# Convolution weights of the second pass: widened on chip from their factors in place of a copy in DRAM

## The chip, the cores and the metric

The kernel runs on one core of a Trainium2 chip. The metric is the device time of one execution in microseconds, given as the median of several runs. The engines are called as in the profile: PE (TensorE matmul), PEld (TensorE weight load), DVE (VectorE), ACT (ScalarE), POOL (GpSimd) and SP (SyncE, which here issues every DMA, in order).

## The reference

Two layers run one after the other on an image `x` of shape (8, 256, 64, 64), all in float32: an attention over reduced keys and values, and a linear attention with a depthwise 5x5 convolution and a grouped 1x1 convolution in front of it. The second layer is what the change is about:

```python
def layer0(x):                       # heads 8, reduction 4
    xr = conv(x, w_sr, stride=4); xr = layernorm over channels
    q = w_q @ x;  k, v = split(w_kv @ xr)
    out = softmax(q k^T / sqrt(32)) v
    return x + gamma_s * (w_out @ out)

def layer1(x):
    qkv = w_qkv @ x                              # 768 channels
    dw  = depthwise 5x5 conv of qkv, padding 2   # w_dw
    agg = grouped 1x1 conv of dw                 # w_pw: 96 groups of 8 -> 8
    ms  = concat(qkv, agg).reshape(B, 64, 24, 4096)   # q, k, v of 8 channels a head
    q, k, v = relu(ms[:, :, :8]), relu(ms[:, :, 8:16]), ms[:, :, 16:]
    kv  = einsum(k, [v, 1]);  out = einsum(q, kv)
    out = out[:-1] / (out[-1:] + 1e-15)
    return x + batchnorm(w_proj @ out)           # 512 -> 256 channels
```

The depthwise and the grouped convolution together are one convolution within groups of 8 channels. Its weights are products: a depthwise tap times an entry of the small 8x8 matrix.

## The kernel before

A tile framework places tiles in pools, sets the semaphores and orders instructions of an engine by a plan of its own, except that those wrapped in `tc.keep_in_program_order` keep their written order. Every DMA goes through SP's queue, in order, with eight completion lanes: a transfer's issue waits for the one issued eight before it.

The kernel has three passes. `first_pass` (0 to about 1981 us) computes the first layer for eight images, 16 steps each, and the `qkv` of the second layer; its loop over `n` (L1056) interleaves by hand. It leaves in DRAM the `planes` (grids of 17x17 cells for the convolution), `kd` and `vd` (keys and values by token) and the image `x2d`. From step 17 on, each step also takes one step of the generator `conv_weights()` (L1112), which loads factors (`wd`, and `wsmall` once for all), forms sums of the four taps a cell (4 to 6 or to 9 variants, `n`), widens them by products on DVE (L698) and writes the wide weights `wt` to DRAM.

`second_pass` (to about 3015 us) runs over 64 units `u = (t, k, b)`: t in 2 halves, k in 4 parts, b in 8 images, with b innermost, so that eight units in a row (a group) share weights. For a unit it does, in the order of L1448 to L1512:

- loads: `load_tokens(u + 1)` (`kq`, 512 KB, and eight pieces of `vq`), in odd units `load_cells_q` (`d0`, two grids of 578 KB for a quad, that is a pair of units), later `load_cells(u + 2)` (`d1`, 578 KB).
- the convolution for keys, `convolve(u, i)` for i = 2, 0, 1: each eight matmuls (sixteen instructions) `cv<-w,c` at L1298 with the weights `w1` of 6 x 128 columns. i = 2 is copied by ACT (`both1`, L1307); for i = 0 and 1 DVE adds (`s`, L1314) and ACT applies the relu (`r`, L1315). Its inputs `c1` come from `paired(u + 1)` (two DVE subs and a copy on POOL), one unit ahead.
- the convolution for queries, `product(m, i, j)` for a quad of two units, nine products (`Q_ORDER`) over two units, two units later; inputs `across` (`c0`) and `down` (`y`), weights `w0` in two tiles: `w0_4` used in even units, `w0_5` in odd ones. The sums run on DVE, the relus on ACT.
- the sums for keys and values: `summed_raw`, `summed(u - 1)`, `ended_raw` and `ended`, with `reduced` (`red_raw`, `red_agg`, L1278 to L1280) on POOL ahead of the small matmuls L1408 and L1420.
- at the end `positive(u + 1)`: the relu of the next `kq` on ACT.

The weights `w1` of the next group come by four loads of 384 KB in its third to sixth unit (L1508); those of the queries by four and five loads of 256 KB at the end of the first two units of a group (L1511), after the old ones have been used. `third_pass` (to 3643 us) divides and projects; its first loads (`raw`) are issued in the last units.

Of the kernel before, what the change touches and what calls it, by code (L numbers as in the profile page):

```python
# [32 lines left out]
P = 128  # L33
# [533 lines left out]

def phase(dy, dx):

    return dy // 2 * 8 + dx // 2 * 4 + dy % 2 * 2 + dx % 2  # L570
# [4 lines left out]
def first_pass(ctx: ExitStack, tc: tile.TileContext, a, fine, planes, x2d, kd, vd, wtd):  # L575
# [7 lines left out]
    made = ctx.enter_context(tc.tile_pool(name="made", bufs=1))  # L583
# [19 lines left out]
    def load(src, name):  # L603
        consts[name] = (nilpool if name == "wsmall" else const).tile(list(src.shape), F32, tag=name, name=name)
        nc.sync.dma_start(consts[name], src)
# [24 lines left out]
    def load_consts():  # L630
        for n, src in (
            ("wq", a.w_q), ("wkv", a.w_kv), ("vec", a.vecs), ("gam", a.gamma_s), ("wout", a.w_out),
            ("wqkv", a.w_qkv), ("wsmall", a.w_small),
        ):
            load(src, n)
        combine_weights()
# [35 lines left out]


    def conv_weights():
        for j, half in ((j, half) for j in (2, 3, 0, 1) for half in range(2)):
            n = 6 if j > 1 else 9
            wd = made.tile([P, 8, n, 16], F32, tag="wd", name=f"wd_{j}_{half}", bufs=1)
            src = a.w_big[:, j, 8 * half : 8 * half + 8]
            nc.sync.dma_start(wd[:, :, :4], src.rearrange("p g (n f) -> p g n f", n=4))
            yield  # L680

            tc.keep_in_program_order(nc.vector.tensor_add(wd[:, :, 4:6], wd[:, :, 0:4:2], wd[:, :, 1:4:2]))
            if n == 9:
                tc.keep_in_program_order(nc.vector.tensor_add(wd[:, :, 6:8], wd[:, :, 0:2], wd[:, :, 2:4]))
                tc.keep_in_program_order(nc.vector.tensor_add(wd[:, :, 8], wd[:, :, 4], wd[:, :, 5]))
            for i in range(8):
                g = 8 * half + i
                w = made.tile([P, n, P], F32, tag="wb", name=f"wb_{j}_{g}", bufs=1)
                small_w = consts["wsmall"][:, j, g]
                if n == 6:  # L690
                    v = w.rearrange("p n (f o) -> p (n f) o", o=D1)
                    big = wd[:, i].rearrange("p n f -> p (n f)").unsqueeze(2).to_broadcast([P, n * 16, D1])
                    small_w = small_w.unsqueeze(1).to_broadcast([P, n * 16, D1])
                else:
                    v = w.rearrange("p n (o f) -> p n o f", o=D1)
                    big = wd[:, i].unsqueeze(2).to_broadcast([P, n, D1, 16])
                    small_w = small_w.unsqueeze(1).unsqueeze(3).to_broadcast([P, n, D1, 16])
                tc.keep_in_program_order(nc.vector.tensor_tensor(v, big, small_w, ALU.mult))  # L698
                if n == 6:
                    nc.sync.dma_start(wtd[j][:, g], w.rearrange("p n m -> p (n m)"))  # L700
                else:
                    nc.sync.dma_start(wtd[j][:, :, g].rearrange("n p m -> p n m"), w)
                yield
# [318 lines left out]
    weights = conv_weights()  # L1022
# [33 lines left out]
    for n in range(n_all + 6):  # L1056
        now, was = n < n_all, 0 <= n - 1 < n_all
        at = n % 16
        filled = now and n // 16 + 1 < B
        if filled and at == 5 and n > 16:  # L1060
            load_x(n // 16 + 1)
        if filled and at == 6:
            ahead = keys_values(n // 16 + 1)
        if now and at == (10 if n < 16 else 1):
            border(n // 16)

        if now:
            e0 = scores(*order[n], 0, q[n])
        catch_up()
        if was:  # L1070
            p = order[n - 1]
            for kc in range(2):
                valued(*p, kc, es[n - 1][kc])
            counted(*p, ej.pop(n - 1))
            es.pop(n - 1)
        if now:
            es[n] = e0, scores(*order[n], 1, q.pop(n))
            ej[n] = joined(*order[n], *es[n])
        if was:
            copied(*p)  # L1080
            normed(*p)

        products = todo.pop(n, [])
        taps = 2 if filled and 6 <= at < 10 else 0
        for f in products[:3]:
            f()
        if filled and at >= 10:
            next(ahead, None)
        for _ in range(taps):
            next(ahead)  # L1090
        if 0 < n + 1 < n_all:
            if n + 1 not in q:
                q[n + 1] = queries(*order[n + 1])
        for f in products[3:]:
            f()
        if was and p[2]:
            b, s = p[:2]
            pair = [att[b, s, 0], att[b, s, 1]]
            for oc in range(2):
                added(b, s, pair, oc)  # L1100
            if s % 2:
                differences(b, s // 2)
                rest_of = [f for pair in (1, 2, 0) for f in qkv_lazy(b, s // 2, pair)]
                for i, count in enumerate((7, 4, 7, 3)):
                    todo[n + 1 + i] = rest_of[:count]
                    rest_of = rest_of[count:]
        for _ in range(taps):
            next(ahead)
        if filled and at >= 10:
            next(ahead, None)  # L1110
        if n > 16:
            next(weights, None)  # L1112
    for _ in weights:
        pass
# [18 lines left out]
    (0, 0): 0, (0, 2): 1, (2, 0): 2, (2, 2): 3, (0, 1): 4, (2, 1): 5, (1, 0): 6, (1, 2): 7, (1, 1): 8,  # L1133
# [6 lines left out]
def second_pass(ctx: ExitStack, tc: tile.TileContext, a, planes, kd, vd, wtd, kvd, kvg, qd, ahead):  # L1140
    nc = tc.nc
    B = a.x.shape[0]
    def pool(name, bufs=1):
# [6 lines left out]
        pool("mid2"), pool("taps2"), pool("pairs2", 2), pool("sides2", 2), pool("between2", 2), pool("third2"),  # L1150
# [12 lines left out]
    wt, wq, grids, cells, kqs, vqs, quad = {}, {}, {}, {}, {}, {}, {}  # L1163


    def load_weights(u, g):
        t, k, b = units[u]
        if g == 0:
            home = second if k % 2 else first
            wt[t, k] = home.tile([P, 4, 6 * P], F32, tag=f"w1_{k % 2}", name=f"w1_{t}_{k}")  # L1170
        nc.sync.dma_start(wt[t, k][:, g], wtd[2 + t][:, 4 * k + g])

    def load_weights_q(u, which):
        t, k, b = units[u]
        home = w_q.tile([P, len(which), 4, P], F32, tag=f"w0_{len(which)}", name=f"w0_{t}_{k}_{len(which)}")
        for i, ij in enumerate(which):
            nc.sync.dma_start(home[:, i], wtd[t][Q_WEIGHTS[ij], :, 4 * k : 4 * k + 4])
            wq[t, k, ij] = home[:, i]
# [37 lines left out]
    def paired(u):  # L1216
        d = grids[u]
        c = pairs.tile([P, 3, 4, (NB + 1) * NB // 2], F32, tag="c1", name=f"c1_{u}")
        v = c.rearrange("p n g (y x) -> p n g y x", x=NB // 2)
        d0, d1, d2 = (d[:, :, :, i : i + NB - 1 : 2] for i in range(3))  # L1220
        nc.vector.tensor_sub(v[:, 0], d0, d1)
        nc.vector.tensor_sub(v[:, 1], d2, d1)

        nc.gpsimd.tensor_copy(v[:, 2], d1)
        cells[u] = c
# [25 lines left out]
    for g in range(4):  # L1251
        load_weights(0, g)
# [37 lines left out]
    def convolve(u, i):  # L1290
        t, k, b = units[u]
        c, w = cells[u], wt[t, k]
        ps = bank("cv", f"cv1_{u}_{i}", 5)
        for g in range(4):
            for da in range(2):
# [4 lines left out]
                    c[:, i, g, cols],  # L1300
# [144 lines left out]

    positive(0)
    paired(0)
    for u in range(n_all + 3):  # L1448
# [16 lines left out]
        if conv and u % 2 == 0:  # L1465
            across(q // 2, 0)
            down(q // 2, 1)
        if now:
            convolve(u, 2)
        if u + 1 < n_all:  # L1470
            paired(u + 1)
# [8 lines left out]
        products(u, 0)  # L1480
        if now:
            convolve(u, 0)
        if conv and u % 2 == 0:
            down(q // 2, 0)
            across(q // 2, 2)
        products(u, 1)
        if now:
# [3 lines left out]
        if now:  # L1491
            ended_raw(u)
            convolve(u, 1)
        if u + 2 < n_all:
            load_cells(u + 2)
        if u == 0:
            load_tokens(2)
            load_weights_q(0, Q_ORDER[:4])
            load_weights_q(0, Q_ORDER[4:])
# [320 lines left out]
def kernel_body(ctx: ExitStack, tc: tile.TileContext, a, out):  # L1820
# [21 lines left out]
    wtd = [scratch(f"wt_{j}", [P, 16, 6 * P] if j > 1 else [9, P, 16, P]) for j in range(4)]  # L1842

    first_pass(tc, a, fine, planes, x2d, kd, vd, wtd)
    with ExitStack() as held:
        top = held.enter_context(tc.tile_pool(name="top3", bufs=1, side="right"))
        ahead = third_pass(held, tc, a, planes, x2d, kvd, kvg, qd, out, top)
        second_pass(tc, a, planes, kd, vd, wtd, kvd, kvg, qd, ahead)
# [125 lines left out]
```

## Time and profile before

| what | value |
|---|---|
| median of 3 runs | 3652.02 us (3647.74 to 3656.05) |
| the profiled execution, its own time | 3644.77 us |
| its span in the profile | 3642.9 us |
| mean granted TensorE clock | 0.986 |
| DMA over the span | 706.47 MB, mean 194 GB/s |
| second pass, copies `both1` of units 0 to 3 | 1985.4, 1993.1, 2011.5, 2030.6 us |
| the same, units 11, 12 | 2150.4, 2175.9 us |
| the same, units 19, 20 | 2278.1, 2301.1 us |
| the same, units 27, 28 | 2401.9, 2425.2 us |
| the same, units 59, 60, 61, 62, 63 | 2902.5, 2915.3, 2937.6, 2953.3, 2968.3 us |
| clock records at 0.5 within the second pass, from | 1976.8, 2004.1, 2021.2, 2171.3, 2297.6, 2543.4, 2792.6, 2918.9, 3000.8 us |

The starts of L1307 are the clock of the second pass: one a unit, in order, so that the distance of two is the time of a unit. Busy shares over the whole span mix three passes with different limits; only windows within a pass tell what limits it. A DMA share near 1 means that all 16 DMA engines have a packet under way.

### The profile page before, as it was taken

The numbers are of one execution on the slowest core, as the hardware profiler recorded it, in microseconds if no ns is written. First come the engines' busy times: TensorE is split into PE (matmuls) and PEld (weight loads), VectorE is DVE, ScalarE is ACT, GpSimd is POOL, SyncE is SP. The second block draws the span as 40 slices with busy tenths as digits, with TensorE's granted clock in tenths as the row PEclk, the third lists the DMA queues.
The fourth block names the chain that finished last, engine by engine and source line by source line (L and its number), as shares of the span: only waits on it lengthen the run. The fifth ranks groups of instructions, "written<-read, shape, count | busy, mean of one in ns | idle before, by whom it ended". The sixth has DMA issues, their size and how long they took to land.

```text
span 3642.9 us, 64216 instructions
## 1 busy us (share of the span) xinstructions
PE 3544.9 (97%) x24738; PEld 1944.9 (53%) x24738; DVE 2270.6 (62%) x3395; ACT 1319.4 (36%) x2729; POOL 1544.4 (42%) x1490
## 2 busy tenths in 40 slices
PE   8999999999999999999998999999999999999998
PEld 4443534434435344344334888888888873333333
DVE  1567576576685766655766767676776684454442
ACT  2445344453453443544443222222322323333322
POOL 2434343344342433433443656565665541222222
PEclk9999999999999999999999999999999998999999
DMA  5346546555575564443465999999999988787773
GB/s 181 101 109 170 149 123 180 145 164 161 141 197 152 136 197 134 134 132 100 124 172 144 292 276 272 286 288 276 279 288 284 273 243 238 217 238 229 219 216 98
DMA packets 629449, 706.47 MB, mean 194 GB/s; under 512 B 81680, under 2 KB 487696, under 8 KB 629136
## 3 DMA queue, kind: packets, MB, share of 16 engines
q1 hardware_dynamic: 629136, 702.29, 67.9%
q8 instruction: 197, 3.23, 0.4%
q14 instruction: 116, 0.95, 0.1%
HBM read 421.44 MB, written 280.69 MB: 193 GB/s over the span
## 4 chain that ended last, share of the span: by engine, by line
PE 85%; DMA 8%; DVE 2%; SPq 1%; POOL 1%; issue 1%; ACT 1%; POOLq 0%; DVEq 0%; ACTq 0%
PE qkv L929 16%; PE p L1697 11%; PE cv L1298 8%; PE sc L807 7%; PE av L831 6%; PE o L885 6%; PE q L792 6%; PE sr L719 6%; PE cv L1329 6%; PE sums L1384 5%; PE den L851 3%; DMA vq<-v 2%; DMA d<-planes 2%; DMA raw<-planes 2%; PE rep L1683 2%
## 5 line engine op out<-in xcount | busy, mean ns | idle before, releaser
L844 POOL TENSOR_TENSOR ej<-e,e 128x512 f32<-128x512 f32 x512 | 682.1, 1360 | 940.4 <-ACT e L813 940.4
L813 ACT ACTIVATE e<-sc 128x512 f32<-128x512 f32 x1024 | 529.3, 608 | 577.0 <-PE sc L807 577.0
L1298 PE MATMUL cv<-w,c 128*128 128x128 f32 x3072 | 392.9, 283 | 21.6 <-DVE s L1314 9.5
L1298 PEld LDWEIGHTS cv<-w,c 128*128 128x128 f32 x3072 | 370.9, 198 | 24.0 <-DVE s L1314 16.1
L1707 POOL TENSOR_TENSOR y<-z,xs 128x512 f32<-128x512 f32 x128 | 165.6, 1302 | 455.6 <-ACT z L1705 426.3
L807 PE MATMUL sc<-q,kk 32*128 32x512 f32 x2048 | 292.9, 639 | 0.0
L929 PE MATMUL qkv<-differences,combined 128*128 128x512 f32 x576 | 291.3, 597 | 0.5 <-POOL differences L902 0.4
L1315 ACT ACTIVATE r<-s 128x512 f32<-128x512 f32 x128 | 80.8, 631 | 547.2 <-DVE s L1314 519.7
L1384 PE MATMUL sums<-vq,r 128*32 128x288 f32 x4096 | 265.2, 407 | 1.4 <-issue 1.4
L1697 PE MATMUL p<-raw,wp 128*128 128x512 f32 x512 | 247.1, 604 | 7.5 <-ACT z L1705 7.4
L831 PE MATMUL av<-e,vv 128*32 128x512 f32 x2048 | 249.4, 598 | 0.6 <-ACT e L813 0.6
L719 PE MATMUL sr<-x,wsr 128*128 128x256 f32 x1024 | 234.6, 383 | 12.2 <-DMA wsr<-in_w_sr_dram 12.1
L792 PE MATMUL q<-x,wq 128*128 128x512 f32 x512 | 242.2, 594 | 0.0
L1697 PE MATMUL p<-agg,wp 128*128 128x512 f32 x512 | 240.4, 592 | 0.0
L719 PEld LDWEIGHTS sr<-x,wsr 128*128 128x128 f32 x1024 | 195.5, 192 | 66.1 <-issue 31.2
L885 PE MATMUL o<-att,wout 128*128 128x512 f32 x512 | 230.4, 592 | 0.0
L864 DVE STREAM_TRANSPOSE rden<-den 128x512 f32<-128x512 f32 x128 | 90.8, 710 | 208.2 <-PE den L851 202.8
L1329 PE MATMUL cv<-y,w 128*128 128x128 f32 x1536 | 205.9, 282 | 11.9 <-DVE y L1248 11.0
L945 DVE TENSOR_TENSOR whole<-part,qkv 128x512 f32<-128x512 f32 x256 | 172.6, 684 | 67.3 <-ACT part L991 47.2
L800 ACT COPY q<-q 128x512 f32<-128x512 f32 x128 | 75.1, 586 | 372.7 <-PE q L792 372.7
L1329 PEld LDWEIGHTS cv<-y,w 128*128 128x128 f32 x1536 | 189.6, 196 | 14.8 <-issue 9.4
L1384 PEld LDWEIGHTS sums<-vq,r 128*32 128x32 f32 x4096 | 155.1, 110 | 76.9 <-issue 2.8
(159 smaller groups left out, 5632.8 us busy)
## 6 DMA issues: line engine op xcount, KB each, us to landing
planes<-stage SPq DMA_DIRECT2D x128, 578.0 KB
d<-planes SPq DMA_DIRECT2D x128, 578.0 KB
vq<-v SPq DMA_DIRECT2D x256, 256.0 KB
raw<-planes SPq DMA_DIRECT2D x64, 578.0 KB
x<-in_xp_dram SPq DMA_DIRECT2D x64, 512.0 KB
wsr<-in_w_sr_dram SPq DMA_DIRECT2D x128, 256.0 KB
x<-x SPq DMA_DIRECT2D x128, 256.0 KB
k<-turned SPq DMA_DIRECT2D x256, 128.0 KB
```

The lines of the kernel that those rows point to most:

```text
L719: nc.tensor.matmul(ps[:, oc], w[:, ci, oc * P : (oc + 1) * P], strips(b, f // 2)[:, ci, f % 2 * NK : (f % 2 + 1) * NK], start=(f == ci == ...
L792: nc.tensor.matmul(ps, consts["wq"][:, ci, c * P : (c + 1) * P], strips(b, s)[:, ci], start=(ci == 0), stop=(ci == 1),)
L807: nc.tensor.matmul(scs[h], kks[b][rows, c, kc * P : (kc + 1) * P], qs[rows], start=True, stop=True)
L813: nc.scalar.activation(e, scs[h], AF.Exp, scale=D0**-0.5)
L831: nc.tensor.matmul(sums["av"][cols], vvs[b][:, kc, c * P + h * D0 : c * P + (h + 1) * D0], es[h], start=(kc == 0), stop=(kc == 1),)
L844: nc.gpsimd.tensor_tensor(e, es0[h], es1[h], ALU.add)
L885: nc.tensor.matmul(ps, consts["wout"][:, c, oc * P : (oc + 1) * P], att[c], start=(c == 0), stop=(c == 1))
L929: nc.tensor.matmul(ps, w, x, start=True, stop=True)
L1298: nc.tensor.matmul(ps[:, g * P : (g + 1) * P], c[:, i, g, cols], w[:, g, n * P : (n + 1) * P], start=(da == 0), stop=(da == 1),)
L1329: nc.tensor.matmul(out, w[:, g], x, start=True, stop=True)
L1384: nc.tensor.matmul(ps[h * D0 : (h + 1) * D0, : 36 * D1].rearrange("p (r n e) -> p r n e", r=3, e=D1), kt[:, par, h, 2 * r + c], vq[:, r : ...
L1697: nc.tensor.matmul(as_block(ps, i // 2), wp[:, i, oc * P : (oc + 1) * P], block(g, i // 2, i % 2, j), start=(i == 0), stop=(i == 3),)
```

## The change

The scratch `wt` in DRAM goes, with `conv_weights()`, the load of `wsmall` and all loads `w<-wt`. The second pass now loads the factors of a group (`factors`: `wd` 128 KB in runs of 256 B, `ws` 16 KB in runs of 128 B a partition and part), adds the variants on DVE, and widens them into `w1` and `w0` in place: `widened_k` by 32 activations with a scale from memory, `widened_q`, for each of two tiles, by one product on DVE, one on POOL and 16 activations. A list `chores` holds these generators, and `do(n)` takes n steps of the first at five points of each unit; a unit takes up to 24 steps where b is 1 or 2 (and in units 0 and 1), else 8.

```diff
+def factors(nc, home, a, j, k, n):
+    wd = home.tile([P, 4, n, R * R], F32, tag=f"wd_{n}", name=f"wd_{j}_{k}")
+    ws = home.tile([P, 4, D1], F32, tag=f"ws_{n}", name=f"ws_{j}_{k}")
+    nc.sync.dma_start(wd[:, :, :4], a.w_big[:, j, 4 * k : 4 * k + 4].rearrange("p g (n f) -> p g n f", n=4))
+    nc.sync.dma_start(ws, a.w_small[:, j, 4 * k : 4 * k + 4])
+    across = wd[:, :, n - (2 if n == 6 else 3) :][:, :, :2]
+    nc.vector.tensor_add(across, wd[:, :, 0:4:2], wd[:, :, 1:4:2])
+    if n == 9:
+        nc.vector.tensor_add(wd[:, :, 4], wd[:, :, 1], wd[:, :, 3])
+        nc.vector.tensor_add(wd[:, :, 5], wd[:, :, 0], wd[:, :, 2])
+        nc.vector.tensor_add(wd[:, :, 8], wd[:, :, 6], wd[:, :, 7])
+    return wd, ws
+
+def widened_k(tc, w, wd, ws):
+    nc = tc.nc
+    for g in range(4):
+        v = w[:, g].rearrange("p (n o) -> p o n", o=D1)
+        for o in range(D1):
+            tc.keep_in_program_order(
+                nc.scalar.activation(
+                    v[:, o], wd[:, g].rearrange("p n f -> p (n f)"), AF.Copy, scale=ws[:, g, o : o + 1]
+                )
+            )
+            yield
+
+def widened_q(tc, w, wd, ws):
...
+    for g in (2, 3):
+        (nc.vector if g == 2 else nc.gpsimd).tensor_tensor(
+            w[:, :, g].rearrange("p n (o f) -> p n o f", o=D1),
+            wd[:, g].unsqueeze(2).to_broadcast([P, n, D1, R * R]),
+            ws[:, g].unsqueeze(1).unsqueeze(3).to_broadcast([P, n, D1, R * R]),
+            ALU.mult,
+        )
+        yield
+    for g in (0, 1):
+        for o in range(D1):
+            tc.keep_in_program_order(
+                nc.scalar.activation(
+                    w[:, :, g, o * R * R : (o + 1) * R * R], wd[:, g], AF.Copy, scale=ws[:, g, o : o + 1]
+                )
+            )
+            yield
...
-    def conv_weights():
-        for j, half in ((j, half) for j in (2, 3, 0, 1) for half in range(2)):
...
-                tc.keep_in_program_order(nc.vector.tensor_tensor(v, big, small_w, ALU.mult))
-                if n == 6:
-                    nc.sync.dma_start(wtd[j][:, g], w.rearrange("p n m -> p (n m)"))
-                else:
-                    nc.sync.dma_start(wtd[j][:, :, g].rearrange("n p m -> p n m"), w)
-                yield
...
-        if n > 16:
-            next(weights, None)
-    for _ in weights:
-        pass
+        if now and n >= n_all - 40:
+            next(ready, None)
```

The first group's `w1` is widened in the last 40 steps of the first pass (`ready`), into a pool `kept` that both passes share. In the second pass the pool `pairs` goes from two buffers to one, and `c1` becomes three tiles, one for each i:

```diff
-        pool("mid2"), pool("taps2"), pool("pairs2", 2), pool("sides2", 2), pool("between2", 2), pool("third2"),
+        pool("mid2"), pool("taps2"), pool("pairs2"), pool("sides2", 2), pool("between2", 2), pool("third2"),
...
+    chores = []
+    def do(n):
+        for _ in range(n):
+            if chores and next(chores[0], chores) is chores:
+                chores.pop(0)
...
+        if u < 2:
+            chores.append(weights_q(0, u))
+        if now:
+            t, k, b = units[u]
+            if 1 <= b < 3 and u > B:
+                chores.append(weights_q(u, b - 1))
+            if u + B < n_all:
+                if b in (1, 5):
+                    load_factors(u + B - b, int(b == 1))
+                if b == 3:
+                    chores.append(weights(u + B - b))
+        wide = u < 2 or now and 1 <= units[u][2] < 3
         if now:
             convolve(u, 2)
         if u + 1 < n_all:
-            paired(u + 1)
+            paired(u + 1, 2)
+        do(3 if wide else 2)
...
         products(u, 0)
+        do(3 if wide else 2)
         if now:
             convolve(u, 0)
+        if u + 1 < n_all:
+            paired(u + 1, 0)
...
         products(u, 1)
+        do(3 if wide else 2)
...
             ended_raw(u)
+            do(6 if wide else 2)
             convolve(u, 1)
+        if u + 1 < n_all:
+            paired(u + 1, 1)
...
-            load_weights_q(0, Q_ORDER[:4])
-            load_weights_q(0, Q_ORDER[4:])
...
             positive(u + 1)
-        if now and u + B < n_all and 2 <= units[u][2] < 6:
-            b = units[u][2]
-            load_weights(u + B - b, b - 2)
-        if conv and units[q][2] >= B - 2 and u < n_all:
-            load_weights_q(u - u % 2, Q_ORDER[4:] if u % 2 else Q_ORDER[:4])
+        do(9 if wide else 0)
```

The numbers of the variants in `Q_WEIGHTS` change with the order in which `factors` lays them out.

More of the change, by code (lines that the diff above doesn't have):

```diff
@@ L566, in general @@
         steps(layer1(b, xt))
+def factors(nc, home, a, j, k, n):
[22 more added lines that the diff above has]
+def widened_q(tc, w, wd, ws):
+    nc = tc.nc
+    n = w.shape[1]
+    for g in (2, 3):
[14 more added lines that the diff above has]
+            yield
 def phase(dy, dx):
@@ L574, in first_pass @@
 @with_exitstack
-def first_pass(ctx: ExitStack, tc: tile.TileContext, a, fine, planes, x2d, kd, vd, wtd):
+def first_pass(ctx: ExitStack, tc: tile.TileContext, a, fine, planes, x2d, kd, vd, ready):
     nc = tc.nc
@@ L582, in first_pass @@
     keys = ctx.enter_context(tc.tile_pool(name="keys", bufs=1))
-    made = ctx.enter_context(tc.tile_pool(name="made", bufs=1))
     xpools.append([ctx.enter_context(tc.tile_pool(name=f"xpool1{j}", bufs=1)) for j in range(2)])
@@ L603, in load @@
     def load(src, name):
-        consts[name] = (nilpool if name == "wsmall" else const).tile(list(src.shape), F32, tag=name, name=name)
+        consts[name] = const.tile(list(src.shape), F32, tag=name, name=name)
         nc.sync.dma_start(consts[name], src)
@@ L632, in load_consts @@
             ("wq", a.w_q), ("wkv", a.w_kv), ("vec", a.vecs), ("gam", a.gamma_s), ("wout", a.w_out),
-            ("wqkv", a.w_qkv), ("wsmall", a.w_small),
+            ("wqkv", a.w_qkv),
         ):
@@ L671, in border @@
             tc.keep_in_program_order(nc.sync.dma_start(v[1 : NB2 + 1, i], src[:NB2]))
-    def conv_weights():
-        for j, half in ((j, half) for j in (2, 3, 0, 1) for half in range(2)):
[L676 to L679, printed above, removed]
-            yield
[L682 to L689, printed above, removed]
-                if n == 6:
-                    v = w.rearrange("p n (f o) -> p (n f) o", o=D1)
-                    big = wd[:, i].rearrange("p n f -> p (n f)").unsqueeze(2).to_broadcast([P, n * 16, D1])
-                    small_w = small_w.unsqueeze(1).to_broadcast([P, n * 16, D1])
-                else:
-                    v = w.rearrange("p n (o f) -> p n o f", o=D1)
-                    big = wd[:, i].unsqueeze(2).to_broadcast([P, n, D1, 16])
-                    small_w = small_w.unsqueeze(1).unsqueeze(3).to_broadcast([P, n, D1, 16])
-                tc.keep_in_program_order(nc.vector.tensor_tensor(v, big, small_w, ALU.mult))
-                if n == 6:
-                    nc.sync.dma_start(wtd[j][:, g], w.rearrange("p n m -> p (n m)"))
-                else:
-                    nc.sync.dma_start(wtd[j][:, :, g].rearrange("n p m -> p n m"), w)
-                yield
     kks, vvs = {}, {}
@@ L1018, in qkv @@
         return [p1, p2, p6, p7, p4, p5, p3]
-    weights = conv_weights()
     new_x(0)
@@ L1132 @@
 Q_WEIGHTS = {
-    (0, 0): 0, (0, 2): 1, (2, 0): 2, (2, 2): 3, (0, 1): 4, (2, 1): 5, (1, 0): 6, (1, 2): 7, (1, 1): 8,
+    (0, 0): 0, (0, 2): 1, (2, 0): 2, (2, 2): 3, (1, 2): 4, (1, 0): 5, (0, 1): 6, (2, 1): 7, (1, 1): 8,
 }
@@ L1139, in second_pass @@
 @with_exitstack
-def second_pass(ctx: ExitStack, tc: tile.TileContext, a, planes, kd, vd, wtd, kvd, kvg, qd, ahead):
+def second_pass(ctx: ExitStack, tc: tile.TileContext, a, planes, kd, vd, kept, first_w, kvd, kvg, qd, ahead):
     nc = tc.nc
@@ L1162, in second_pass, with weights, weights_q @@
     n_all = len(units)
-    wt, wq, grids, cells, kqs, vqs, quad = {}, {}, {}, {}, {}, {}, {}
-    def load_weights(u, g):
+    wt, wq, parts, grids, cells, kqs, vqs, quad = {}, {}, {}, {}, {}, {}, {}, {}
+    wt[0, 0] = first_w
+    def weights(u):
         t, k, b = units[u]
[L1168 to L1173, printed above, removed]
-        t, k, b = units[u]
[L1175 to L1178, printed above, removed]
+        home = second if k % 2 else kept
+        w = wt[t, k] = home.tile([P, 4, 6 * P], F32, tag=f"w1_{k % 2}", name=f"w1_{t}_{k}")
+        return widened_k(tc, w, *parts.pop((2 + t, k)))
+    def weights_q(u, part):
+        t, k, b = units[u]
+        wd, ws = parts[t, k]
+        n = 5 if part else 4
+        w = w_q.tile([P, n, 4, P], F32, tag=f"w0_{n}", name=f"w0_{t}_{k}_{n}")
+        for ij, i in Q_WEIGHTS.items():
+            if (i < 5) == (part == 1):
+                wq[t, k, ij] = w[:, i % 5]
+        return widened_q(tc, w, wd[:, :, :5] if part else wd[:, :, 5:], ws)
     def load_cells(u):
@@ L1212, in load_tokens, with paired @@
         vqs[u] = vq.rearrange("p r (c f h e) -> p r c f h e", c=6, f=4, h=4)
-    def paired(u):
+    def paired(u, i):
         d = grids[u]
-        c = pairs.tile([P, 3, 4, (NB + 1) * NB // 2], F32, tag="c1", name=f"c1_{u}")
-        v = c.rearrange("p n g (y x) -> p n g y x", x=NB // 2)
+        c = cells[u, i] = pairs.tile([P, 4, (NB + 1) * NB // 2], F32, tag=f"c1_{i}", name=f"c1_{u}_{i}")
+        v = c.rearrange("p g (y x) -> p g y x", x=NB // 2)
         d0, d1, d2 = (d[:, :, :, i : i + NB - 1 : 2] for i in range(3))
[L1221 to L1225, printed above, removed]
+        if i == 2:
+            nc.gpsimd.tensor_copy(v, d1)
+        else:
+            nc.vector.tensor_sub(v, d2 if i else d0, d1)
     def across(m, j):
@@ L1249, in down @@
         nc.gpsimd.tensor_tensor(v[:, 1], c2, c1, ALU.subtract)
-    for g in range(4):
-        load_weights(0, g)
     load_cells(0)
@@ L1291, in convolve @@
         t, k, b = units[u]
-        c, w = cells[u], wt[t, k]
+        c, w = cells[u, i], wt[t, k]
         ps = bank("cv", f"cv1_{u}_{i}", 5)
@@ L1299, in convolve @@
                     ps[:, g * P : (g + 1) * P],
-                    c[:, i, g, cols],
+                    c[:, g, cols],
                     w[:, g, n * P : (n + 1) * P],
@@ L1444, in products, with load_factors @@
             product(m, *ij)
+    chores = []
[3 more added lines that the diff above has]
+                chores.pop(0)
+    def load_factors(u, what):
+        t, k, b = units[u]
+        j = t + 2 * what
+        parts[j, k] = factors(nc, kept if what else w_q, a, j, k, 6 if what else 9)
     positive(0)
-    paired(0)
+    load_factors(0, 0)
+    for i in (2, 0, 1):
+        paired(0, i)
     for u in range(n_all + 3):
@@ L1467, in second_pass @@
             down(q // 2, 1)
+        if u < 2:
+            chores.append(weights_q(0, u))
+        if now:
+            t, k, b = units[u]
+            if 1 <= b < 3 and u > B:
[6 more added lines that the diff above has]
+        wide = u < 2 or now and 1 <= units[u][2] < 3
         if now:
@@ L1841, in kernel_body, with ready @@
     qd = [scratch(f"q_{b}", [C, R * R, NK]) for b in range(B)]
-    wtd = [scratch(f"wt_{j}", [P, 16, 6 * P] if j > 1 else [9, P, 16, P]) for j in range(4)]
-    first_pass(tc, a, fine, planes, x2d, kd, vd, wtd)
     with ExitStack() as held:
-        top = held.enter_context(tc.tile_pool(name="top3", bufs=1, side="right"))
-        ahead = third_pass(held, tc, a, planes, x2d, kvd, kvg, qd, out, top)
-        second_pass(tc, a, planes, kd, vd, wtd, kvd, kvg, qd, ahead)
+        with tc.tile_pool(name="kept", bufs=1) as kept:
+            first_w = kept.tile([P, 4, 6 * P], F32, tag="w1_0", name="w1_0_0")
+            def ready():
+                yield from widened_k(tc, first_w, *factors(nc, kept, a, 2, 0, 6))
+            first_pass(tc, a, fine, planes, x2d, kd, vd, ready())
+            top = held.enter_context(tc.tile_pool(name="top3", bufs=1, side="right"))
+            ahead = third_pass(held, tc, a, planes, x2d, kvd, kvg, qd, out, top)
+            second_pass(tc, a, planes, kd, vd, kept, first_w, kvd, kvg, qd, ahead)
         next(ahead)
```

## Prediction

> **What bounds the kernel now.** I read the page's busy shares first, then the slices for the second pass (about 1981 to 3015 us), then windows inside that pass, PE's waits and the chain of waits through one stall.
>
> ```profile
> PE 3544.9 (97%) x24738; PEld 1944.9 (53%) x24738; DVE 2270.6 (62%) x3395; ACT 1319.4 (36%) x2729; POOL 1544.4 (42%) x1490
> ...
> DMA  5346546555575564443465999999999988787773
> GB/s 181 101 109 170 149 123 180 145 164 161 141 197 152 136 197 134 134 132 100 124 172 144 292 276 272 286 288 276 279 288 284 273 243 238 217 238 229 219 216 98
> ```
>
> PE is busy 97% overall, so only its gaps can be won. DMA fills from slice 22 on: the second pass moves some 280 GB/s with its engines 90% or more busy, and nothing else in the kernel comes near. The windows (time, then busy us of PE, PEld, DVE, ACT, POOL, the granted clock, DMA share, GB/s) show two regimes:
>
> ```profile
> 2188.00:2278.00 90.00, 88.63 (x1300) 77.69 (x1299) 67.05 (x112) 26.01 (x39) 54.52 (x52) 1.00 0.94 273
> 2278.00:2302.00 24.00, 20.91 (x254) 18.79 (x253) 15.22 (x22) 6.18 (x10) 12.77 (x11) 0.91 1.03 306
> 2302.00:2402.00 100.00, 100.00 (x1480) 87.41 (x1480) 73.25 (x128) 28.53 (x44) 60.33 (x59) 0.99 0.98 281
> 2402.00:2426.00 24.00, 20.66 (x327) 18.34 (x329) 14.99 (x22) 6.17 (x10) 12.53 (x11) 1.00 1.03 290
> ```
>
> For 100 us PE is full; then 24 us hold a hole, with the DMA share at 1.03. The pass has 64 units, eight to a group that shares weights. The copies `both<-cv` of L1307, one a unit, start at 2175.9, 2301.1, 2425.2, 2550.6, 2673.8 and 2797.7 for units 12, 20, 28, 36, 44 and 52: a group takes 123.2 to 125.4 us. Between holes a pair of units takes 29.37 us (13.73 + 15.64, units 24 to 26), so eight would take 117.5. The long unit is always the fourth (unit 19: 23.0; unit 27: 23.3; unit 35: 26.9). What ended that hole:
>
> ```profile
> 2400.05 7.57 DMA vq<-v
> 2407.64 7.45 DMA d<-planes
> 2415.21 0.17 DVE c L1233
> 2415.38 1.04 issue
> 2416.42 2.04 DVE y L1248
> 2418.46 1.71 DVE c L1233
> ...
> 2421.68 0.68 DVE s L1314
> 2422.44 2.03 PE cv L1298 x16
> ```
>
> PE waits for DVE, but DVE had waited for the quad's grid `d0` (`d<-planes`), which stood behind `vq` in the queue. The chain thus goes through two transfers, not through arithmetic. After it, PE follows itself without a gap until 2484. In the list of DMA issues the transfers at stake are:
>
> ```profile
> w<-wt SPq DMA_DIRECT2D x72, 256.0 KB
> wt<-wb SPq DMA_DIRECT2D x32, 384.0 KB
> w<-wt SPq DMA_DIRECT2D x32, 384.0 KB
> ```
>
> **The change, part by part.**
> (1) *DMA out of the second pass.* A group loads 4 x 384 + 9 x 256 KB = 3.93 MB. In the packet records of 2301 to 2425, 512 packets of 3072 B at 0.155 us and 1152 of 2048 B at 0.113 us, over 16 engines, are 5.0 + 8.1 = 13.1 us of 124.1 at a share of 0.986 (122.4 busy). (By bytes, 3.93 MB at 281 GB/s is 14.0.) In their place come two `wd` loads (512 packets of 256 B each, 0.018 us in the first pass's records of the old `wd`) and two `ws` (128 packets each of 128 B, put at the same 0.018 us): 1280 x 0.018 / 16 = 1.4 us. New demand: 122.4 - 13.1 + 1.4 = 110.7 us a group, 94% of 117.5. That 94% suffices is shown by the window 2188 to 2278: share 0.94, PE without a wait, six units in 89.9 us (14.98 each).
>
> The Trainium skill, "DMA: Bandwidth & Descriptors", Specifications, gives 512 B as the least transfer for line rate, with read-modify-write below it; it speaks against the new loads. No run here shows that for reads into SBUF; were their time doubled, the demand would be 112.1 us, still under 117.5.
>
> (2) *The holes.* From unit 3 (2030.6) to unit 63 (2968.3) 937.7 us pass; 60 x 14.68 = 880.8, so 56.9 us stand above PE's own rate. With DMA under demand they could all go. I leave 17: the last three pieces of each q part stand on ACT between the relu of `kq` and the next copy `both1`, and the products that read `w0` wait for them, some 1.0 us in unit 2 and 0.2 us in unit 3 of a group, seven times: 8; 4 at units 58 to 61, where the third pass's `raw` loads (64 x 578 KB begin there) stay; 5 for evictions that come late behind a chore. Gain 40. Bounds: 52 (only the end stays) and 20 (case B below).
>
> (3) *ACT, DVE, POOL.* Each group adds 32 activations of 128x96 and 32 of 128x64 or 128x80, two products each on DVE and POOL, and five adds on DVE. Rows for the sizes:
>
> ```profile
> L800 ACT COPY q<-q 128x512 f32<-128x512 f32 x128 | 75.1, 586 | 372.7 <-PE q L792 372.7
> ...
> L876 ACT ACTIVATE copy<-one 128x16 f32<-128x16 f32 x128 | 29.8, 233 | 0.0
> ...
> L775 ACT COPY kk<-k 128x256 f32<-128x256 f32 x16 | 6.0, 372 | 20.5 <-PE k L772 20.5
> ```
>
> Between 16 and 256 columns: 0.233 + 80/240 x 0.139 = 0.28 us; bounds 0.23 and 0.59, since a strided output and a scale from memory are not in these rows. 64 x 0.28 = 18 us a group beside ACT's 28.5% (33.5 us): 44% busy. The crowded units (second and third of a group, 16 q pieces) need 16 x 0.28 = 4.5 us over a base of 4.1 to 5.7, of 14.68. So hidden, behind PE. DVE: the old products took 951 ns for 768 columns and 1351 for 1152, 1.04 ns a column beyond 150 ns: 0.68 and 0.82 us, and five adds at 0.2 to 0.4, 3.0 us on 86 of 117.5. POOL: 512-column products take 1.3 to 2.1 us, so two add 3 to 5 us to 71 of 117.5; `red_agg` and `red_raw` stand behind them with 1 to 2 us in hand before L1408 and L1420 wait. If that cover goes, up to 2 us a group.
>
> The Trainium skill, "ScalarE: Activation LUTs", What ACT_TABLE_LOAD costs, prices an activation at 186 ns + 0.833 ns a column, some 93 ns more for a pointer operand. That estimate is 359 ns for 96 columns and would make 64 pieces 22 us instead of 18; hidden either way, but the sums above do not use it.
>
> (4) *First pass.* Eight loads, 64 products (73.6 us on DVE by the rows 32 x 951 and 32 x 1351) and sixteen adds go, with 64 writes `wt<-wb` (31.5 MB). PE is back to back there: batches of 16 steps take 242.59 us with this work and without it. Two took 244.83, as `sr` waited for `wsr` at 1105.3 (1.0 us) and 1350.2 (2.0), loads queued among those writes on SP. Gain 4 (bounds 0 to 4.5). The first 32 activations run in the last 40 steps: ACT is idle 577 us before L813 waiting for PE, so 32 x 0.28 = 9 us go into that; bound 0 to 8 lost if they delay `e`.
>
> (5) *Start of the second pass.* Now PE waits 6.2 us for the turned tokens, then 4.4 for `d0`, 4.0 for `red_agg` and others up to unit 3, with the clock at 0.5 for 10.2, 6.8 and 3.4 us. Removed: 1.5 MB of `w1` loads ahead of the first grids and 2.25 MB of `w0` ahead of `d0`, and one pair of subs (1.9 us) from in front of unit 0's first sum. Added: `wd`, `ws` on SP behind the first loads, and 32 chores on ACT (9 us) in units 0 and 1, ahead of units 1 and 2's relus of `kq`; POOL's two `w0` products stand ahead of `red_agg`. The 6.2 us stay, as they wait for the first pass. I take 4 gained, bounds 15 gained (all waits up to unit 3 that `w` loads lie behind) and 5 lost.
>
> (6) *`pairs` from two buffers to one, in three tiles.* A sub for unit u+1 now waits for `convolve(u, i)` to have read its tile. The next use is a unit (14.7 us) later against 0.95 us on DVE: nothing; if DVE falls a whole part late, 1 us a unit of part (2)'s bounds. The third pass is unchanged.
>
> Sum: 40 + 4 + 4 = 48 us off. Against the profiled 3644.8 us (span 3642.9, the rest lies around it) 3596.8; the median of the runs is 7.2 us above the profiled execution, so 3652 - 48 = **3604 us**. By the bounds of all terms: 52 + 4.5 + 15 = 71.5 off (3580) to 20 + 0 - 5 - 8 = 7 off (3645).
>
> **Rivals.**
> *A, the forecast:* 3604.
> *B, half:* the hole shrinks but stays in the fourth unit: `d0` is issued in an odd unit behind `kq` and eight `vq` loads and lands 15 us later, whatever the weights. For: the chain shows `vq` 7.57 and `d` 7.45 us in line. Against: units at share 0.94 have no hole. About half of 56.9 goes, 25 with start and first pass: 3627.
> *C, slower:* ACT's order. Chores sit in one in-order queue ahead of `both1`, the `r` relus and `kq`'s; at 0.59 us each (the 128x512 row, if strided outputs and pointers cost so much) 9 chores at a wide unit's end are 5.3 us ahead of the next copy, in two units a group: 10.6 us, and a half clock for 6.8 us after it loses another 3.4: 14 a group against 7 to 8 saved. From 65/7 = 9.3 us a group (56.9 + 8 over seven groups) the kernel is slower; at 14 it is 7 x 14 = 98 against 65: 3685. For: ACT is in order and PE's banks only five. Against: rows say 0.28, and a relu's reader comes a unit later.
> *D, hidden anyway:* the holes belong to the order of `d0`, `y` and `c0` on DVE; without weights, DMA idles and they stay: 3645 to 3652. Against: the chain.
>
> **How the numbers follow.** A 0.60, B 0.21, D 0.06, C 0.13. A measurement tells 0.2% (7.3 us) from no change. Faster: A and B with a little of D, 0.82; same: most of D, 0.05; slower: C, 0.13. The range leaves out C and the far end of A: 3588 to 3640, which holds B and most bounds above.
>
> **What would show it.** `w<-wt` is gone and the DMA share is 0.90 to 0.96 in the second pass; units 12 to 52 come 117 to 120 us apart a group, the fourth unit is no longer the long one, and the dips to clock 0.5 every 124 us are gone (A). A fourth unit of 18 to 20 us behind `d<-planes` is B; PE waiting for ACT `w0` or `both` for over 9 us a group is C; periods of 124 at a share of 0.9 are D. ACT's pieces should show 0.23 to 0.37 us; above 0.5 I am wrong on part (3). `sr` should not wait for `wsr` at 1105 and 1350. I am wrong on the whole if the excess of 56.9 us from unit 3 to unit 63 does not fall by half.

## The result and the profile after

The changed kernel takes 3618.89 us in the median of four runs (3616.2 to 3620.4) against 3649.88 (3646.2 to 3656.1) before: 31 us less, ratio 0.9913 with a 95% interval of 0.9895 to 0.9930. Once more on another occasion: 3622.79 against 3654.52, ratio 0.991 (0.9894 to 0.9927). The forecast was 48 us less. It has the sign and the mechanism; a third of the expected gain is missing.

The profiled execution of the changed kernel has a span of 3618.3 us. First the page: the busy shares, and the slices of DMA.

```profile
PE 3536.7 (98%) x24738; PEld 1937.9 (54%) x24738; DVE 2221.5 (61%) x3371; ACT 1461.8 (40%) x3241; POOL 1525.8 (42%) x1506
...
DMA  5345445455454454553645999999999977787773
```

DVE lost 49 us (the old products less the new ones), ACT gained 142. In the slices DMA still shows 9 through the second pass, as before: the tenths are too coarse to tell the change. The windows inside the pass tell it (time, busy us of PE, PEld, DVE, ACT and POOL, the clock, DMA share, GB/s):

```profile
2164.00:2284.00 120.00, 118.59 (x1738) 104.50 (x1737) 89.55 (x155) 51.37 (x116) 73.34 (x72) 1.00 0.94 261
2284.00:2404.00 120.00, 118.60 (x1738) 104.48 (x1737) 92.66 (x156) 53.06 (x118) 72.06 (x72) 1.00 0.92 262
2404.00:2524.00 120.00, 116.28 (x1704) 102.04 (x1703) 89.95 (x154) 50.48 (x114) 70.52 (x68) 0.99 0.92 258
```

The share is 0.92 to 0.94, where the groups before had 0.96 to 0.99; PE is idle 1.4 us in 120 (3.7 in the third window), and ACT is 43% busy where it was 28%. Groups of eight units (starts of units 12, 20, 28, 36, 44, 52) now take 120.8, 119.2, 121.8, 120.5 and 119.1 us; they took 123.3 to 125.3. The fourth unit of a group is no longer long. The second is: 18.05 us from unit 17 to 18, 18.04 from 25 to 26, 22.05 from 33 to 34; with the third it takes 31.05 us at units 17 and 41, where a pair without a hole takes 29.37. PE's waits from 1930 to 3030 (total, times, longest) say why:

```profile
PE cv L1344 <- ACT w L611: 12.1, 8, 2.7
PE cv L1313 <- DVE stage L959: 6.7, 1, 6.7
PE cv L1313 <- DVE s L1329: 5.8, 2, 3.0
PE cv L1344 <- DVE y L1265: 4.1, 3, 2.1
```

No DMA is named any more. The first line is the wait that the change brought: products of the query convolution (L1344) wait for a piece of their weights from ACT (L611). The second is the wait for the first pass, 6.2 us before. The third lies at units 9 and 33. The pieces themselves, by shape (busy us and mean ns of one):

```profile
L590 ACT ACTIVATE w<-wd,ws 128x96 f32<-128x96 f32 x256 | 91.1, 463 | 0.0
...
L611 ACT ACTIVATE w<-wd,ws 128x80 f32<-128x80 f32 x128 | 35.4, 349 | 1.8 <-DMA kq<-k 1.8
...
L611 ACT ACTIVATE w<-wd,ws 128x64 f32<-128x64 f32 x128 | 33.4, 335 | 0.1
L601 DVE TENSOR_TENSOR w<-wd,ws 128x512 f32<-128x512 f32 x8 | 12.3, 1543 | 0.0
```

The span by stretches, from the starts of `both1` in both profiles:

| stretch | before | after | difference |
|---|---|---|---|
| start to unit 0 | 1985.4 | 1980.7 | -4.7 |
| unit 0 to 3 | 45.2 | 43.1 | -2.1 |
| unit 3 to 63 | 937.6 | 910.6 | -27.0 |
| unit 63 to the end | 674.7 | 684.0 | +9.3 |

### The profile page after: what moved, and what is told of

Read it like the earlier page. It is cut to its first block, busy times and chain, and to the rows that moved or that the text cites. A ratio compares the mean times of both kernels' runs of the same rounds, so it can differ in the third digit from the quotient of the medians.

```text
span 3618.3 us, 64503 instructions
## 1 busy us (share of the span) xinstructions
PE 3536.7 (98%) x24738; PEld 1937.9 (54%) x24738; DVE 2221.5 (61%) x3371; ACT 1461.8 (40%) x3241; POOL 1525.8 (42%) x1506
## 4 chain that ended last, share of the span: by engine, by line
PE 87%; DMA 6%; DVE 3%; ACT 1%; SPq 1%; issue 1%; POOL 0%; POOLq 0%; DVEq 0%; ACTq 0%
PE qkv L946 16%; PE p L1740 11%; PE cv L1313 8%; PE sc L824 8%; PE av L848 7%; PE o L902 6%; PE q L809 6%; PE sr L736 6%; PE cv L1344 6%; PE sums L1399 6%; PE den L868 3%; DMA raw<-planes 2%; DMA vq<-v 2%; PE rep L1726 2%; PE den L1707 1%
## 5 line engine op out<-in xcount | busy, mean ns | idle before, releaser
L1344 PE MATMUL cv<-y,w 128*128 128x128 f32 x1536 | 204.0, 278 | 6.9 <-DVE y L1265 4.1
L946 PE MATMUL qkv<-x,wqkv 128*128 128x512 f32 x384 | 188.8, 611 | 5.2 <-ACT e L830 5.2
## 6 DMA issues: line engine op xcount, KB each, us to landing
k<-turned SPq DMA_DIRECT2D x256, 128.0 KB
```

The costliest lines, as they stand in the source:

```text
L946: nc.tensor.matmul(ps, w, x, start=True, stop=True)
L1344: nc.tensor.matmul(out, w[:, g], x, start=True, stop=True)
```

## The experiments

**Is it the weights' transfers?** The first kernel is the one before without the loads of later weights; it adds no work on chip.

```diff
     def load_weights(u, g):
         t, k, b = units[u]
+        if u:
+            wt[t, k] = wt[0, 0]
+            return
...
     def load_weights_q(u, which):
         t, k, b = units[u]
+        if u:
+            for ij in which:
+                wq[t, k, ij] = wq[0, 0, ij]
+            return
```

> The kernel before, with the weights of the first group loaded once and used for all 64 units: the loads w<-wt of the other seven groups (27.5 MB) are left out, so the convolutions of later groups use wrong weights; nothing else is changed, and no activation or product is added. Theory A (the holes in the fourth unit are a debt of the DMA queues): groups take 117.5 to 119 us in place of 124, the fourth unit is no longer the long one, DMA share in the pass falls to about 0.93, time about 3600 to 3612 (38 to 50 us below before). Rival B (d0 is late behind kq and vq whatever the weights): a fourth unit of 18 to 20 us stays, about 3627. Rival D (the holes belong to DVE's order): 3645 to 3652. The distance of this run to the changed kernel (3619) is what the widening on chip costs: theory A says 8 to 18 us.

It took 3601.41 us against 3651.02, ratio 0.987 (0.9841 to 0.9899). Groups take 117.1 to 117.9 us up to unit 52; the last, in which the third pass's loads begin, takes 127.6, with a hole in unit 57. One group of it, as a window:

```profile
2282.00:2400.00 118.00, 118.00 (x1734) 104.06 (x1733) 88.62 (x149) 35.03 (x54) 72.97 (x69) 1.00 0.94 263
```

PE is busy for all of the 118 us, at a DMA share of 0.94 (the transfers `vq` and `d`, which stood in the chain before, are all there, but no longer late). So the holes up to unit 52 were the debt of the queues, that is of transfers asked for faster than they land: B and D fall. Units 3 to 63 take 891.7 us here; the changed kernel takes 910.6. In these two profiles the work on chip costs the difference, some 19 us, where I had allowed 13 (8 and 5).

**And if the loads come back?** The changed kernel with loads that nothing reads, five of 96 KB a unit:

```diff
+    def load_spare(u):
+        if B <= u + 5 and u < n_all - B:
+            i = nth[0] % 20
+            nth[0] += 1
+            d = spare.tile([P, 192], F32, tag="spare", name="spare")
+            nc.sync.dma_start(d, x2d[0][:P, i * 192 : i * 192 + 192])
```

> The changed kernel with loads that nothing reads: five of 96 KB in each unit from the third to the 56th (3.93 MB a group, as much as the weights of before), from DRAM into four small tiles, spread evenly over the unit. Nothing waits for them but the queue. Theory A (debt by sum): demand 110.7 + 13 = 124 us a group against 117.5, so groups take 122 to 127, DMA share 0.97 or more, and the time is 30 to 45 us above the changed kernel, 3650 to 3665. Rival (the holes came from the bunch of nine loads in two units, not from the sum): groups stay at 119 to 120.5, time within 8 us of 3619.

It took 3685.75 us, ratio to before 1.0096 (1.0065 to 1.0127); groups take 128.0 to 131.5 us. A group's window, and PE's waits from 2015 to 2930:

```profile
2298.00:2429.00 131.00, 123.71 (x1732) 107.78 (x1728) 90.21 (x155) 50.66 (x117) 72.09 (x70) 0.97 0.96 267
```
```profile
PE cv L1344 <- DVE y L1265: 25.7, 15, 3.7
PE raw L1423 <- POOL red_raw L1295: 15.7, 10, 3.2
```

The bunch of loads was not the cause: spread out, the same bytes cost more, not less. By the packet records the engines are busy 126.0 of 131.3 us (the spare loads, in packets of 768 B, take 14.4 of them; the weights before took 13.1). That is more than the 117.5 that PE needs, so the sum of the transfers decides again; that a group takes 131 and not 126 I had not expected. PE waits for `y` and `red_raw`, whose inputs `d0` and `kq` come by DMA. That the four small tiles hold up SP's queue, since the fifth load waits for the first, may have a part in it; it was not tried apart.

**Is it the order on ACT?** The hole in the second unit, in ACT's timeline of the changed kernel at unit 26 (start, us, what, idle before):

```profile
2371.25 0.69 ACT L1350 ACTIVATE r<-side 128x512 f32<-128x512 f32 x1 [1.51 <-DVE side L1372]
2371.83 1.03 ACT L1300 ACTIVATE kq<-kq 128x1024 f32<-128x1024 f32 x1
2372.77 0.81 ACT L611 ACTIVATE w<-wd,ws 128x64 f32<-128x64 f32 x3
2373.49 0.56 ACT L1322 COPY both<-cv 128x512 f32<-128x512 f32 x1
```

and PE beside it:

```profile
2370.73 1.50 PE L1313 MATMUL cv<-w,c 128*128 128x128 f32 x12
2373.63 1.06 PE L1344 MATMUL cv<-d,w 128*128 128x128 f32 x6 [1.40 <-ACT w L611]
```

The last three pieces (L611) could have run in the 1.5 us in which ACT waited before `r`; they stand in order behind `r` and the relu of `kq` (L1300), and PE goes on 0.05 us after the third. The edit takes three more steps ahead of that relu:

```diff
-        do(3 if wide else 2)
+        do(4 if wide else 2)
```

at the first three points of a unit.

> The changed kernel with four steps of chores in place of three at the first three points of a crowded unit, so that all 18 steps of a q part are issued ahead of the relu of the next kq. Theory (the hole between the second and third unit of each group is ACT's order: three pieces behind that relu): PE's waits on ACT w fall from 12.1 us to under 2, groups from 119.2 to 117.5 to 118, time 10 to 14 us below the changed kernel, about 3606. Rival (the hole belongs to the products as such: they come late because w0 is free only after the last product of the old group): the waits stay at 10 or more and the time within 3 us of 3619.

3607.55 us (3596.9 to 3613.3), ratio to before 0.9885 (0.9849 to 0.9921): 11 us below the changed kernel's median, though the intervals of the two ratios overlap. In the trace it is plain; PE's waits from 2015 to 2930 now begin with

```profile
PE cv L1313 <- DVE s L1329: 4.5, 5, 2.5
PE cv L1344 <- DMA d<-planes: 3.4, 1, 3.4
PE raw L1423 <- POOL red_raw L1295: 1.9, 4, 0.6
```

and no line names ACT `w`. The groups still take 116.9 to 123.0 us.

**Does ACT's work itself cost?** Each activation twice:

```diff
+            for _ in range(2):
                 tc.keep_in_program_order(nc.scalar.activation(...))
```

> The changed kernel with each widening activation issued twice, to the same output: ACT gets 512 more of them, some 160 us. Theory A (ACT's work is hidden but for the three pieces ahead of the third unit of a group): the hole there grows from 1.3 us by three more pieces (0.85 us), 7 to 8 times, and the time by 5 to 12 us, to about 3627. Rival C (chores ahead of evictions in ACT's queue cost everywhere): units 3 to 8 of a group lengthen too, groups from 119 to 124 or more, time 3650 or more.

3620.04 us (3612.8 to 3627.0) against 3618.89 and 3622.79 of the changed kernel: nothing. The page has 512 pieces of 96 columns, and 256 each of the others:

```profile
L591 ACT ACTIVATE w<-wd,ws 128x96 f32<-128x96 f32 x512 | 203.7, 467 | 6.8
```

ACT is busy 73.9 us from 2284 to 2404 where it was 53.1, and C's lengthening of all units is not there. The smaller loss that theory A expected, 5 to 12 us, doesn't show in the time either. PE's waits on ACT `w` are 6.4 us, less than before the doubling, though others grew (DVE `s` 8.1, ACT `kq` 3.4), and units 3 to 63 take 918.0 us, within the 910.6 and 919.0 of the changed kernel's two profiles. The seven pairs of a second and a third unit (from units 9, 17 and so on to 57) take 239.9 us in all, against 229.4 and 238.6 in those two profiles, so that a small loss at the hole itself can't be excluded. The rest of ACT's time is covered; what matters is which piece stands behind what.

**The hole at unit 33.** There the chain of waits of the changed kernel goes through another load, of the second half of the taps:

```profile
2470.05 8.43 DMA taps<-in_w_taps_dram
2478.49 0.02 issue
2478.50 6.75 DMA d<-planes
...
2486.66 1.95 DVE y L1265
2488.62 2.29 DVE c L1250
```

It is issued among the pieces of `vq`, ahead of the second grid of `d0`. The next kernel keeps the chores early and loads the taps in four parts:

```diff
-        if was and p == n_all // 2 - 1:
-            load_taps(1)
+        if u in (20, 22, 24, 36):
+            load_taps(1, (20, 22, 24, 36).index(u))
```

> As the kernel with the chores early (3607.6), and the second half of the taps (576 KB) in four tiles that are loaded at units 20, 22, 24 and 36 in place of one load at unit 32. Theory (the hole of 2.5 us at unit 33, with 3.4 us of half clock, comes from that load ahead of the grid d0): the hole goes, 3 to 5 us less, 3602 to 3605; PE's idle time at unit 33 is under 0.5 us. Rival (the hole is DVE's, crowded where t changes): it stays, and the time is within 2 us of 3607.6.

3604.03 us, ratio to before 0.986 (0.9843 to 0.9876); the changed kernel, run beside it, 3622.79. The hole at unit 33 is gone, with its record of half clock (3.4 us at 2487.0 with the chores early alone; none from 2017 to 2880 here). Both edits together give 18.8 us, and here the intervals are apart. Against the chores early alone the gain of 3.5 us is within the spread. The kernel of the first experiment has the same load of the taps and no hole at unit 33 (15.62 and 13.74 us from there): the load costs something only beside the work on chip.

**The changed kernel again**, for the last stretch:

> The changed kernel as it is, once more, to see how far the last stretch (from unit 63 to the end) moves from one execution to the next. If its 683.9 us in the first profile, 9.3 more than before the change, belong to the change, they come again within 2 us; if they are scatter, the stretch is at 673 to 680, as in the other runs with the same third pass. Time 3616 to 3622.

3622.79 us. The last stretch took 678.9 us, not 684.0. Over all profiles of the study, in which the third pass is the same, it lies between 673.2 and 686.6 us. So most of the 9.3 us in the table above is scatter (in these two profiles 6.6 us of it have arisen some 150 us into the stretch, where the records of half clock are 34.1 us long against 27.3). Without that line the table gives 33.8 us less; the medians give 31. The same kernel's units 3 to 63 took 919.0 us this time, with waits of PE of 1.4 to 5.0 us around the end of each second unit.

**Is the rest DVE's queue?** DVE's part of each product moved to eight more activations, and the first four points of a crowded unit take 6, 6, 6 and 7 steps, so that all 25 stay ahead of the relu:

```diff
-    for g in (2, 3):
-        (nc.vector if g == 2 else nc.gpsimd).tensor_tensor(
+    for g in (3,):
+        nc.gpsimd.tensor_tensor(
...
-    for g in (0, 1):
+    for g in (0, 1, 2):
```

> As the one before, and the product of each q part that DVE made (1.3 to 1.55 us each) made by eight more activations on ACT. Theory (what is left of the chores' cost, 902.6 - 891.7 = 11 us from unit 3 to 63, is DVE's queue in the two crowded units: PE waits 4.5 us on DVE s): PE's waits on DVE in units 4 to 57 go under 1 us and the time falls by 3 to 6 us against the one before. Rival C (ACT's queue is the tight one): PE waits on ACT w or both, and the time rises by 3 to 10 us.

3606.43 us (3596.0 to 3610.9) against 3604.03, while its profile (the fastest of the four) had units 3 to 63 in 892.6 us against 904.3. That left it open, so both ran again, side by side:

> The kernel with chores and taps early, once more, beside the next one on the same chip. It should be at 3601 to 3607, with groups of 118 to 122 us.

> The kernel without DVE's part in the products, once more: 3606.4 in four runs that reached from 3596 to 3611 left open whether DVE's queue costs anything. Theory (DVE in the crowded units is the rest of the chores' cost): median 3 to 6 us below the one before in this call, units 3 to 63 in 890 to 896 us against 902 to 906. Rival (nothing in it; the first profile was a lucky execution): medians within 2 us, and units 3 to 63 in 900 us or more.

3597.45 us (ratio to before 0.9875, 0.9855 to 0.9895) and 3597.55 us (0.9872, 0.9851 to 0.9893). Units 3 to 63 took 894.1 us with DVE's part, and 899.7 without. The theory falls: DVE's products cost nothing that can be measured, though each takes 1.3 to 1.5 us, and what I had read as the rest of the chores' cost is within the spread of single executions (904.3 and 894.1 for one kernel). The ratios say the same of the whole: 0.986 and 0.9875 with the weights made on chip, 0.987 in the first experiment, which adds no work on chip but keeps writes that cost the first pass 4.5 us (below). What the widening still costs is no more than the spread.

**The first pass.** The kernel of the first experiment, without the writes that nothing reads then; all products stay:

```diff
-                if n == 6:
+                if g > 3 or j not in (0, 2):
+                    pass
+                elif n == 6:
```

> As the kernel before without later weight loads (3601.4), and without the writes wt<-wb that nothing reads then: 56 of 64 are left out, and the eight for the first group stay, with all products on DVE. Theory (the two long batches of the first pass come from loads of wsr queued among these writes, not from DVE's work): all batches from the second on take 242.6 us, the two that took 244.8 among them, and the first pass ends 4.4 us sooner. Rival (DVE's products delay them): the two long batches stay at 244.8.

All batches from the second on take 242.58 to 242.60 us, by the starts of the products `o`; with the writes, two take 244.63 and 244.90. The wait that the kernel of the first experiment, with the writes, shows from 100 to 1930 us,

```profile
PE sr L719 <- DMA wsr<-in_w_sr_dram: 2.8, 2, 2.0
```

is not there without them. The 73.6 us of DVE's products hid all along; the writes did not. (One run, 3603.54 us; its last stretch was 686.6 us, the longest of all, so its time tells nothing of 4 us.)

## Why the prediction was right in kind and short in size

- *The bound and the debt:* right. Demand by the packet records is 0.922 x 119.2 = 109.9 us a group against 110.7 forecast, and 0.94 is enough (first experiment). The packets of 256 B took 0.018 us each in the second pass too. The Trainium skill, "DMA: Bandwidth & Descriptors", Specifications, puts the least transfer for line rate at 512 B. A packet of 256 B in 0.018 us is 14 GB/s for an engine, one of 2048 B in 0.113 us 18, so some of the rate is lost, but 1.2 us a group is all that these packets take; whether they are read and modified first no run here shows.
- *First pass:* 4 forecast, 4.5 measured between the starts of the first and last batches, and the cause shown.
- *Start:* 4 forecast, 2.3 measured (6.8 at unit 3, less 4.5). PE's wait for `red_agg`, 4.0 before, is 4.1 after.
- *The holes, the step that was mis-sized:* "I leave 17", for a gain of 40. The excess from unit 3 to 63 fell from 56.9 to 29.8 us, and the gain was 27. Of the 29.8, 7.9 lie before unit 12, 14.3 from there to unit 52 and 7.6 behind it, where the forecast left 4 for the end. The forecast put the three pieces behind the relu at 1.0 us in the second unit of a group and 0.2 in the third, 8 in all. The place was right. The size was not: PE waited 12.1 us, 0.7 to 2.7 us at a time; at unit 26 `r` came late ahead of the same relu, and the pieces took 0.335 us in place of 0.28. At units 9 and 33 (taps ahead of `d0`) a wait for another late input, DVE's `s`, came just before it; the two together were 3.5 and 3.7 us. A record of half clock, 3.4 us long, follows each of these, and a third the wait of 2.7 us at unit 59. By half of their length, an estimate, the three cost 5 us, and the 17 had no term for them. Changing both orders gives 18.8 us: the missing gain, and a kernel (ratio to before 0.986 and, again, 0.9875) that beats both.
- *ACT's cost:* 64 x 0.28 = 18 us a group forecast; 20 measured (160 over eight). Hidden, as doubling it showed. Of the test in the prediction (0.23 to 0.37 us a piece) the 96-column pieces fail at 0.463.
- *DVE's products:* 0.68 and 0.82 us forecast, 1.54 and 1.27 measured; no effect on the time that can be measured.
- *The single buffer of `pairs`:* nothing forecast. It was not tried apart; the kernels with both orders changed come within the spread of the first experiment, which has two buffers, so that it can have cost a few microseconds at most.
- *Rivals:* The time alone does not choose: 3619 is nearer to B's 3627 than to the forecast's 3604. B and D fell with the first experiment, and B's fourth unit of 18 to 20 us is not there (15.6 to 17.3). C has the right place, an ordered queue with a late reader, and the wrong price: 12 us of waits in all, not 14 a group.
- *The last test of the prediction,* that it is wrong on the whole if the excess does not fall by half, goes narrowly against it: the excess fell by 48% in the first profile, and by 33% (to 38.2 us) in the second. The reason is not the one that the test was meant for, a debt that stays: with both orders changed and the weights still made on chip, the excess is 23.5 and 13.3 us, 59% and 77% less.

## What to carry to other kernels

Where DMA runs at its limit for a whole pass, as here at a share of 0.96 to 0.99, look whether weights that are a product of small factors can be made on chip in place of fetched. ACT, busy 28% of this pass, was the place, as long as each piece was issued ahead of anything on its queue that waits. Count the waits by what stands in front of the last piece, not by the busy time of all: here doubling the work cost nothing that can be measured, and moving three pieces and one load gained 18.8 us. A stretch that two kernels share is worth a look in a second execution before a difference in it is explained.

## What was not expected of the hardware

The 96-column activations, whose output has a stride of eight elements, took 463 ns, those of 80 and 64 columns, with runs of 16, 349 and 335. The Trainium skill, "ScalarE: Activation LUTs", What ACT_TABLE_LOAD costs, states 186 ns + 0.833 ns a column, and 93 ns for a pointer operand. The estimate from it for 64 and 80 columns is 332 and 346 ns, which agrees; for 96 it is 359, which does not; that the stride makes the 104 ns of difference was not tried apart. The product on DVE took 1.54 us for 512 columns and 1.27 for 640, more for the smaller one, while products of 768 took 0.951 us in the first pass. In the trace POOL is busy, mostly with `red_agg`, for all but 0.08 us of each of the sixteen new products, while 60 of the 64 old ones ran with POOL idle. That speaks for POOL as the cause; against it, the other four ran beside POOL for up to 0.37 us and took no longer, and without DVE's part POOL's own pieces took the same (1.14 against 1.15 us for 512 columns). So whether the two hinder each other stays open.
